# A state-space scan kernel on one Trainium2 core: a fourth product buffer, a later addition, fewer products in PSUM, and fp8 weights rounded once

## The chip, the cores and the metric

The kernel runs on one core of a Trainium2 chip. The metric is device time in microseconds (us) of one execution, and the number compared is the median of several runs. The engines are named as in the profile: PE is TensorE (matmuls and transposes; PEld its weight loads), DVE is VectorE, ACT is ScalarE, POOL is GpSimd, SP is SyncE, which issues the DMAs here. Each engine takes its instructions in the order in which they were queued for it; they wait for each other through semaphores.

## What is computed

The input is x of shape (4, 64, 64, 96) in float32. Four layers follow each other.

- Layer 0 adds to x a two-dimensional selective scan (SS2D) of the group-normalized x: a projection to 192 channels and a gate, a 3x3 depthwise convolution with SiLU, then a state-space scan along four directions (rows, columns, and both reversed), and at the end LayerNorm, the gate and a projection back.
- Layer 1 does the same on the real and imaginary parts of the two-dimensional Fourier transform of x (64 x 33 frequencies, 384 inner channels), image by image, transforms back and adds x.
- Layers 2 and 3 treat the pixels as tokens: attention without a softmax (6 heads), and a feed-forward network whose inputs, weights and biases are rounded to an 8-bit float (5 exponent bits, 2 mantissa bits).

The scan is what matters here. For each direction, channel and one of 16 states n it is

```
dA = jnp.exp(dl[..., None] * A)
hst = hst * dA + (dl * ul)[..., None] * bl[:, :, None, :]
y = jnp.einsum('bkdn,bkn->bkd', hst, cl)
```

so a recurrence along the sequence, for every state, and then a sum over the 16 states of h times C.

## The kernel before

**Pieces.** The scan work is cut into phases: two groups of two images each for layer 0 (g0, g1), and four single images for layer 1 (b0 to b3). A phase holds four directions, each cut into segments along the sequence (eight of 512 elements in layer 0; 512, 512, 384, 384 and 320 in layer 1). There are 144 segments, 64 and 80. In a segment, the 16 states are taken four at a time (q from 0 to 3), and within each q come three chunks of 128 channels (c from 0 to 2). So a segment has twelve steps, and the kernel 1728. `scans` (L524) writes them out in a fixed order for PE, DVE, ACT and POOL; nothing reorders them afterwards.

**One step.** A step `st` computes four states' recurrences (scans 0 to 3, each one DVE instruction, L710), multiplies each by C, and adds the four products up in PSUM, together with those of the other q.

- The factors exp(delta*A) come from ACT: for scans 0 and 1 into SBUF, one step ahead (`front_x`), for scans 2 and 3 into PSUM (`front_y`; both through L682).
- The inputs delta*u*B of scans 0 and 1 are scaled by ACT in transposed form (`make_bx`, L646) and turned by PE into PSUM (`transposed`, L678). Those of scans 2 and 3 are made by POOL (`front_b`, L700), one step ahead, in rows 1 and 2 of a tile h of 3 x 512 elements. A ring of three PSUM banks (`room`, L671) serves these tiles.
- The scan writes either over its input in PSUM, and is then called kept, or into a row of h. `Step.kept` (L519) says which: scan 0 always, and scan 3 too in every other step. Kept results are multiplied by C on DVE (`multiply_kept`, L728) into a tile hk, and ACT copies their last column as the state for the next segment (`keep_state`, L735). All others are multiplied on POOL in one instruction of two or three rows (`multiply`, L747, after the state copy of L744), one step later.
- PE adds products up with transposes that accumulate in PSUM (`accumulate`, L757): `add_kept` for hk, and `add_rest` for the rows of h that POOL multiplied. `add_rest` of a step comes two steps later, at the head of that step (L871). `close_chunk` (L783) copies the sum out once the last q is in.

h has three buffers (L698). `front_b` for the next step is queued on POOL in the middle of a step, behind `multiply` of the step before.

The order of a step (L871 to L910), with each call's engine: add_rest of two steps ago (PE); add_kept 3 of the last step (PE); scan 0 (DVE); front_y 2 and front_x of the next step (ACT); multiply_kept 0 (DVE); add_kept 0 (PE); front_y 3 (ACT); multiply of the last step and front_b of the next (POOL); scan 1 (DVE); a slot; transposed 0 of the next step (PE); scan 2 (DVE); a slot; transposed 1 of the next step (PE); scan 3 (DVE), and its multiply_kept if it is kept; a slot.

**Side work.** Everything else is cut into small pieces that the three slots of a step take (L820) at a rate fixed for each phase (`RATES`, L27: 2.85 pieces a step in layer 1). That is the projections and convolutions of later phases (`Block`), the Fourier transforms (L1033, L1089), the outputs of earlier phases, and `tokens` (L1156), which does layers 2 and 3 of an image while the next image is scanned. The last image's tokens run after the scans, in a wider form. `tokens` loads its weights for every image: float32 tiles by DMA (L1183), of which w1, w2, b1 and b2 of each layer are then rounded to fp8 on DVE (L1189); b1 and b2 are turned back to float32 (L1191). Its `norm_all` (L1205) has two buffers for the squares (L1240). The projection loads hold both halves of a weight chunk (`wi`).

**Broadcasts.** B and C are spread over the partitions by DMAs on SP (`fetch_b`, `fetch_c`, L624), once for each q.

Of the kernel before, what the change touches and what calls it, by code (L numbers as in the profile page):

```python
# [7 lines left out]
F32 = mybir.dt.float32  # L8
F16 = mybir.dt.float16
F8 = mybir.dt.float8e5  # L10
AF = mybir.ActivationFunctionType
# [7 lines left out]
NB, HH, WW, CH = 4, 64, 64, 96  # L19
# [3 lines left out]
C, P = 3, 128  # L23
SM = 512
LATE, BURST = "late", "burst"

RATES = [1.6, 2.35, 2.85, 2.85, 2.85, 2.85]  # L27
EXP_LN = "natural_log_exp_and_others"


# [95 lines left out]
class Inputs:  # L126


    def __init__(self, blk, sp, xf, chunks, half, nm, w):
        self.blk, self.sp, self.xf, self.half, self.nm, self.w = blk, sp, xf, half, nm, w  # L130
        self.todo = [
            (c, r, n) for c in chunks for p0, p1 in blk.cfg.parts for r, n in blk.rows_of(p0, p1, half == 0)
        ]
        self.ahead, self.wi = [], {}
        for _ in range(2):
            self.load()

    def load(self):
        if not self.todo:
            return  # L140
        sp, cfg, nc = self.sp, self.blk.cfg, self.blk.nc
        c, r, n = self.todo.pop(0)
        if c not in self.wi:
            t = sp.tile([CH, cfg.KI, 2, cfg.PI], F32, name=f"{cfg.pre}_wi_{self.nm}_{c}", tag=f"wi{self.w}", bufs=2)
            nc.sync.dma_start(out=t, in_=self.blk.w["inw"][:, :, :, c, :])
            self.wi[c] = t
        x = sp.tile(
            [CH, 2, 512], F32, name=f"xi{self.half}_{self.nm}_{c}_{len(self.todo)}", tag=f"xin{self.w}", bufs=3
        )
        nc.sync.dma_start(out=x[:, :, : n * 64], in_=self.xf[:, :, r * 64 : (r + n) * 64])  # L150
        self.ahead.append((self.wi[c], x))
# [6 lines left out]
class Block:  # L158
# [44 lines left out]
    def in_proj(self, out, wi, half, xin, n):  # L203

        cfg = self.cfg
        for i in range(cfg.NI):
            for ki in range(cfg.KI):
                if i or ki:
                    yield
                self.nc.tensor.matmul(  # L210
                    out[i * cfg.PI : (i + 1) * cfg.PI, :n],
                    wi[:, ki, half, :],
                    xin[:, max(i, ki), :n],
                    start=(ki == 0),
                    stop=(ki == cfg.KI - 1),
                )
# [171 lines left out]
    def gated(self, E, g, io, out_proj):  # L388
# [7 lines left out]
        with E.pool(f"{cfg.pre}nm{g}") as sp:  # L396
# [15 lines left out]
            def worker(w):  # L412
# [6 lines left out]
                for b, (r, nr) in blocks:  # L419
# [93 lines left out]
class Step:  # L513


    def __init__(self, z, q, c):
        self.z, self.q, self.c = z, q, c
        self.nm = f"{z.nm}_{q}_{c}"
        self.kept = (0, 3) if (C * q + c) % 2 else (0,)  # L519
        self.hk = {}  # L520
        self.px, self.ay = {}, {}


def scans(tc, ctx, phases, ident):  # L524
# [8 lines left out]
    nc = tc.nc  # L533
# [161 lines left out]
    def front_b(st):  # L695

        S = st.z.S
        st.h = sp.tile([P, 3, SM], F32, name=f"h_{st.nm}", tag="h", bufs=3)  # L698
        for j in range(2):
            nc.gpsimd.tensor_tensor(  # L700
                st.h[:, 1 + j, :S], st.z.du[:, st.c, :S], st.z.b[st.q][:, j, :S], ALU.mult
            )
# [96 lines left out]
    with tc.manual_schedule(engines=IN_ORDER):  # L799
# [43 lines left out]
        for i, st in enumerate(steps):  # L843
# [309 lines left out]
NT = LTOK // P  # L1153


def tokens(E, ins, consts, ident, x1, b, out):  # L1156

# [5 lines left out]
    with E.pool(f"tk{b}") as sp:  # L1163
# [10 lines left out]
        def weights(ly):  # L1174

            nm, w, bufs = f"{b}_{ly}", {}, min(W, 2)
            for name, shape in (
                ("wqkv", [A, 3 * CH]), ("wqt", [CH, A]), ("wff", [CH, CH]), ("bff", [A, CH]),
                ("w1", [CH, 4 * CH]), ("w2", [P, 3, CH]), ("b1", [P, 3]), ("b2", [P, CH]),
            ):  # L1180
                t = w[name] = sp.tile(shape, F32, name=f"{name}_{nm}", tag=name, bufs=bufs)
                src = ins[f"l{ly}_{name}"]
                nc.sync.dma_start(out=t, in_=src.to_broadcast([P, CH]) if name == "b2" else src)  # L1183
# [11 lines left out]
        loads = [weights(ly) for ly in (2, 3)]  # L1195
        ws = [next(loads[0])] + ([next(loads[1])] if W > 1 else [])
# [3 lines left out]
        yield  # L1200
        yield
        for load in loads[: len(ws)]:
            yield from load

        def norm_all(nm):  # L1205

# [8 lines left out]
            for i in range(n + 2):  # L1215
# [146 lines left out]
        for ly in (2, 3):  # L1362
            nm = f"{b}_{ly}"
            if len(ws) < ly - 1:
                ws.append(next(loads[1]))
                yield from loads[1]
            q = ws[ly - 2]
            wq = q["wqkv"]
            if W == 1:
# [34 lines left out]
def build(tc, ins, consts, out):  # L1404
    nc = tc.nc
    with ExitStack() as ctx:
# [31 lines left out]
        x1 = [dram.tile([LTOK, CH], F32, name=f"x1_{b}", tag=f"x1_{b}") for b in range(NB)]  # L1438
        single = [dict() for _ in range(NB)]

        def flip0(E, g):
            yield from blk[0].flip(E, g, pairs[g])

# [17 lines left out]
        def end1(E, b):  # L1461
            io = single[b]
            att = dram.tile([HH, WF, 2 * CH], F32, name=f"att_{b}", tag="att", bufs=NB)
            put = out1(att, b)
            yield from blk[1].gated(
                E, b, io, lambda E, *a: put(E, blk[1], *a)
            )
            yield
            rest = tokens(E, ins, consts, ident, x1[b], b, out)
# [136 lines left out]
```

## Time and profile before

| | us |
|---|---|
| median of the 3 runs shown | 11332.17 (11327.04 to 11333.0) |
| the profiled execution's own time | 11308.41 |
| its span in the profile | 11306.6 |
| ahead of the first scan | 217.2 |
| layer 0 scans, g0 and g1 | 2451.0 and 2444.0 |
| layer 1 scans, b0 to b3 | 1469.6, 1425.7, 1469.0, 1435.2 |
| after the last scan (the tail) | 395.0 |

The profile holds one execution; its mean granted TensorE clock is 0.90 of full speed. In that profile the busy time of an engine is the sum of its instructions, and its share is taken of the span. A group puts together the instructions of one line, engine and tile; behind its busy time and mean duration stands the idle time that the engine had just before them, and what released it. The waits are the same idle times sorted by waiting group and releaser, with total, count and longest. A segment's or phase's length is counted from its first scan to the next one's first scan.

### The profile page before, as it was taken

Reading aid. Unit: us, or ns where it says so; the run is one execution under the profiler, and the core shown is the slowest. Engines: PE = TensorE matmul, PEld = TensorE weight load, DVE = VectorE, ACT = ScalarE, POOL = GpSimd, SP = SyncE. Lnnn points to the kernel's source line nnn. Section 1 sums busy time; section 2 is a strip of 40 time slices with the busy share of each in tenths; the row PEclk is TensorE's granted clock in tenths of the full one; section 3 lists DMA queues with packets and bytes.
Section 4 is the critical chain, followed back from the end, with each engine's and each line's share of the span. In section 5 each row is a group of like instructions: output and inputs, shape, how many; then the busy total and the mean of one; then the engine's idle time right before and its main releaser. Section 6 shows DMA issues by size and latency. Waiting matters only on the chain. (4 is left out here: it accounts for less than half of the span.)

```text
span 11306.6 us, 163986 instructions
## 1 busy us (share of the span) xinstructions
PE 9021.5 (80%) x54944; PEld 6600.5 (58%) x54944; DVE 9899.2 (88%) x10695; ACT 9384.7 (83%) x19648; POOL 9405.2 (83%) x7464
## 2 busy tenths in 40 slices
PE   5678788777888888888899888887788777887775
PEld 2555555556666656656676665665566555665554
DVE  6889999889999998999888798989989889889864
ACT  3779999999888998998778788878888788878853
POOL 2999999989988998998788798878888779888750
PEclk9889999889999999999889899998899888998887
DMA  5655555556666556555543545442244223542242
GB/s 146 144 130 130 133 129 123 155 156 153 156 161 140 129 144 140 134 142 169 156 134 119 136 136 157 150 113 94 92 145 138 93 90 107 158 120 94 82 130 38
DMA packets 1208406, 1468.97 MB, mean 130 GB/s; under 512 B 482759, under 2 KB 1020559, under 8 KB 1149063
## 3 DMA queue, kind: packets, MB, share of 16 engines
q1 hardware_dynamic: 1207559, 1458.48, 47.8%
q8 instruction: 434, 7.11, 0.3%
q14 instruction: 413, 3.38, 0.1%
HBM read 1221.74 MB, written 236.50 MB: 129 GB/s over the span
## 5 line engine op out<-in xcount | busy, mean ns | idle before, releaser
L747 POOL TENSOR_TENSOR h_l<-h_l,bc_l 128x1536 f32<-128x1536 f32 (+2 forms) x1728 | 4567.8, 2643 | 184.0 <-DVE h_l L710 68.1
L700 POOL TENSOR_TENSOR h_l<-du_l,bc_l 128x512 f32<-128x512 f32 (+2 forms) x3456 | 3966.7, 1170 | 770.1 <-PE acc_l L757 718.1
L646 ACT ACTIVATE bx_l<-dut_l,bt_l 128x192 f32<-128x192 f32 (+2 forms) x6272 | 2756.4, 499 | 0.3
L757 PEld LDWEIGHTS acc_l<-ident,h_l 128*128 128x128 f32 (+1 forms) x15840 | 2047.7, 155 | 689.2 <-issue 325.9
L757 PE MATMUL acc_l<-ident,h_l 128*128 128x128 f32 (+1 forms) x15840 | 2326.3, 299 | 135.9 <-POOL h_l L747 135.6
L682 ACT ACTIVATE ax_l<-delta_l,l_alog 128x512 f32<-128x512 f32 (+2 forms) x3456 | 2140.4, 667 | 0.0
L710 DVE TENSOR_TENSOR_SCAN h_l<-b_l,state_l,h_l 128x512 f32<-128x512 f32 (+2 forms) x1263 | 1389.1, 1121 | 114.2 <-ACT b_l L682 106.6
L678 PE MATMUL b_l<-ident,bx_l 128*128 128x128 f32 (+1 forms) x6817 | 1200.5, 295 | 227.1 <-DVE h_l L710 220.2
L678 PEld LDWEIGHTS b_l<-ident,bx_l 128*128 128x128 f32 (+1 forms) x6817 | 842.9, 149 | 829.5 <-DVE h_l L710 476.8
L682 ACT ACTIVATE b_l<-delta_l,l_alog 128x512 f32<-128x512 f32 (+2 forms) x1948 | 1221.0, 627 | 107.7 <-DVE k_l L728 32.0
L710 DVE TENSOR_TENSOR_SCAN b_l<-ax_l,state_l,b_l 128x512 f32<-128x512 f32 (+2 forms) x842 | 956.5, 1136 | 194.1 <-PE b_l L678 191.3
L757 PE MATMUL acc_l<-ident,k_l 128*128 128x128 f32 (+1 forms) x5117 | 836.9, 294 | 334.3 <-DVE k_l L728 320.1
L678 PE MATMUL ab_l<-ident,bx_l 128*128 128x128 f32 x5312 | 900.9, 298 | 246.5 <-DVE h_l L710 237.7
L682 ACT ACTIVATE ab_l<-delta_l,l_alog 128x512 f32<-128x512 f32 x1326 | 913.8, 689 | 149.0 <-DVE h_l L710 70.0
L678 PEld LDWEIGHTS ab_l<-ident,bx_l 128*128 128x128 f32 x5312 | 648.5, 151 | 622.2 <-DVE h_l L710 452.4
L710 DVE TENSOR_TENSOR_SCAN h_l<-ax_l,state_l,b_l 128x512 f32<-128x512 f32 (+2 forms) x841 | 951.2, 1131 | 42.1 <-PE b_l L678 40.4
L710 DVE TENSOR_TENSOR_SCAN h_l<-ab_l,state_l,h_l 128x512 f32<-128x512 f32 x743 | 920.2, 1261 | 73.2 <-ACT ab_l L682 46.7
L728 DVE TENSOR_TENSOR k_l<-b_l,bc_l 128x512 f32<-128x512 f32 (+2 forms) x1460 | 895.4, 613 | 50.2
L757 PE MATMUL acc_l<-ident,hk_l 128*128 128x128 f32 x3976 | 641.3, 296 | 328.3 <-DVE hk_l L728 315.5
L757 PEld LDWEIGHTS acc_l<-ident,k_l 128*128 128x128 f32 (+1 forms) x5117 | 627.3, 150 | 437.2 <-DVE k_l L728 368.7
L297 PE MATMUL pc_l<-pad_l,l_dg 128*128 128x512 f32 (+2 forms) x1656 | 783.9, 561 | 57.2 <-ACT uh_l L275 42.9
L757 PEld LDWEIGHTS acc_l<-ident,hk_l 128*128 128x128 f32 x3976 | 494.1, 152 | 409.7 <-DVE hk_l L728 337.3
(252 smaller groups left out, 15015.4 us busy)
## 6 DMA issues: line engine op xcount, KB each, us to landing
bc_l<-l_xd_l SPq DMA_DIRECT2D x640, 512.0 KB
bc_l<-l_xd_l SPq DMA_DIRECT2D x512, 256.0 KB
bc_l<-l_xd_l SPq DMA_DIRECT2D x128, 1024.0 KB
bc_l<-l_xd_l SPq DMA_DIRECT2D x128, 768.0 KB
us_l<-l_u SPq DMA_DIRECT2D x96, 768.0 KB
l_y<-y_l SPq DMA_DIRECT2D x288, 256.0 KB
yt_l<-l_y SPq DMA_DIRECT2D x264, 192.0 KB
yt_l<-l_y SPq DMA_DIRECT2D x128, 384.0 KB
```

The costliest lines, as they stand in the source:

```text
L297: nc.tensor.matmul(pc[:, : n * 64].rearrange("p (r w) -> p r w", w=64), diag[:, t, :], pad[:, r - p0 + dy : r - p0 + dy + n, dx : dx + 64] ...
L646: nc.scalar.activation(t[:n, b, :, ch], z.dut[:n, b, :, ch], AF.Copy, scale=z.bt[:n, b, m : m + 1])
L678: nc.tensor.transpose(pb[:, t : t + n], st.z.bx[st.q, j][:n, b, st.c], ident[:n, :n])
L682: nc.scalar.activation(out, z.delta[:, st.c, : z.S], AF.Exp, scale=z.blk.A[:, st.c, z.k, n : n + 1])
L700: nc.gpsimd.tensor_tensor(st.h[:, 1 + j, :S], st.z.du[:, st.c, :S], st.z.b[st.q][:, j, :S], ALU.mult)
L710: nc.vector.tensor_tensor_scan(h[:, ::step], a[:, ::step], b[:, ::step], 0.0 if z.first else z.state[st.c][:, n : n + 1], ALU.mult, ALU.add,)
L728: nc.vector.tensor_tensor(hk[:, : z.S], kept_at(st, j), z.c[st.q][:, j, : z.S], ALU.mult)
L747: nc.gpsimd.tensor_tensor(h, h, z.c[st.q][:, 1 : 1 + m, : z.S], ALU.mult)
L757: nc.tensor.matmul(z.acc[st.c][:m, b, :], hc[:, t : t + m], ident, start=(first and b == 0), stop=(last and b == 0), is_transpose=True,)
```

## The change

1. h gets a fourth buffer.
2. `add_rest` of the step two back moves from the head of a step to behind the slot after scan 2, ahead of `transposed` 1. Steps that work on the last q (q = 3) of their segment keep theirs at the head (`older.q == NQ - 1`).
3. `Step.kept` takes scan 3 too when `(3q + c) % (2 * KI) == 1`. KI is 1 in layer 0, which leaves every other step there, and 2 in layer 1, where 3 steps of 12 remain of 6. In the others POOL multiplies the third row.
4. The fp8 weights and biases of layers 2 and 3 are loaded and rounded once, by a new side task `quantized`, the last of the first phase, into tiles that stay. `tokens` takes them from there.
5. Smaller tiles and edits that go with it: `wi` holds one half of a weight chunk; the input tiles `xin` are as long as their longest use; `Ln` of the normalization writes in place in PSUM, not to a tile of its own; `lnq` has one buffer; the weights of layer 3 are loaded without a generator; two waits of a slot in `tokens` become six; the rate in layer 1 is 2.82, not 2.85.

The lines of the scans move up by one (L710 becomes L709, for instance).

```diff
-RATES = [1.6, 2.35, 2.85, 2.85, 2.85, 2.85]
+RATES = [1.6, 2.35, 2.82, 2.82, 2.82, 2.82]
...
-        self.ahead, self.wi = [], {}
+        self.ahead, self.wi, self.most = [], {}, 64 * max(n for _, _, n in self.todo)
...
-            t = sp.tile([CH, cfg.KI, 2, cfg.PI], F32, name=f"{cfg.pre}_wi_{self.nm}_{c}", tag=f"wi{self.w}", bufs=2)
-            nc.sync.dma_start(out=t, in_=self.blk.w["inw"][:, :, :, c, :])
+            t = sp.tile([CH, cfg.KI, cfg.PI], F32, name=f"{cfg.pre}_wi_{self.nm}_{c}", tag=f"wi{self.w}", bufs=2)
+            nc.sync.dma_start(out=t, in_=self.blk.w["inw"][:, :, self.half, c, :])
...
-                    ln = sp.tile([P, 512], F32, name=f"ln_{nm}", tag=f"ln{w}")
-                    nc.scalar.activation(ln[:, :n], pv[:, :n], AF.Ln, bias=self.eps)
-                    nc.scalar.activation(pv[:, :n], ln[:, :n], AF.Exp, scale=-0.5)
+                    nc.scalar.activation(pv[:, :n], pv[:, :n], AF.Ln, bias=self.eps)
+                    nc.scalar.activation(pv[:, :n], pv[:, :n], AF.Exp, scale=-0.5)
...
-        self.kept = (0, 3) if (C * q + c) % 2 else (0,)
+        self.kept = (0, 3) if (C * q + c) % (2 * z.cfg.KI) == 1 else (0,)
...
-        st.h = sp.tile([P, 3, SM], F32, name=f"h_{st.nm}", tag="h", bufs=3)
+        st.h = sp.tile([P, 3, SM], F32, name=f"h_{st.nm}", tag="h", bufs=4)
...
-            if older:
+            if older and older.q == NQ - 1:
                 add_rest(older)
...
             slot(None, hold=long)
+            if older and older.q < NQ - 1:
+                add_rest(older)
             if nxt:
                 transposed(nxt, 1)
...
+def quantized(E, cp, ins, quant):
...
+    shapes = (("w1", [CH, 4 * CH]), ("w2", [P, 3, CH]), ("b1", [P, 3]), ("b2", [P, CH]))
+    with E.pool("qw") as sp:
+        loaded = []
+        for ly in (2, 3):
+            for name, shape in shapes:
+                t = sp.tile(shape, F32, name=f"{name}_{ly}", tag=f"{name}{ly}")
+                src = ins[f"l{ly}_{name}"]
+                nc.sync.dma_start(out=t, in_=src.to_broadcast([P, CH]) if name == "b2" else src)
+                loaded.append((ly, name, shape, t))
+        for _ in range(6):
+            yield
+        for ly, name, shape, t in loaded:
+            keep = cp if name in ("w1", "w2") else sp
+            r = keep.tile(shape, F8, name=f"q{name}_{ly}", tag=f"q{name}{ly}")
+            yield LATE
+            nc.vector.tensor_copy(r, t, saturate=False)
+            if keep is sp:
+                r, q = cp.tile(shape, F32, name=f"k{name}_{ly}", tag=f"k{name}{ly}"), r
+                nc.vector.tensor_copy(r, q)
+            quant[ly][name] = r
+    yield
...
-                ("w1", [CH, 4 * CH]), ("w2", [P, 3, CH]), ("b1", [P, 3]), ("b2", [P, CH]),
...
-            yield w
-            for name in ("w1", "w2", "b1", "b2"):
-                t = w[name]
-                r = sp.tile(list(t.shape), F8, name=f"q{name}_{nm}", tag=f"q{name}", bufs=bufs)
-                yield LATE
-                nc.vector.tensor_copy(r, t, saturate=False)
-                if name in ("b1", "b2"):
-                    nc.vector.tensor_copy(t, r)
-                else:
-                    w[name] = r
...
+            w.update(quant[ly])
+            return w
...
-                    sq = sp.tile([P, Q, CH], F32, name=f"lnq_{nm}_{t0}", tag="lnq0", bufs=2)
+                    sq = sp.tile([P, Q, CH], F32, name=f"lnq_{nm}_{t0}", tag="lnq0")
...
-            [(flip0, 0), (begin0, 1), (gate0, 0), (gate0, 1)],
+            [(flip0, 0), (begin0, 1), (gate0, 0), (gate0, 1), (quant0, 0)],
```

More of the change, by code (lines that the diff above doesn't have):

```diff
@@ L143, in load @@
         if c not in self.wi:
-            t = sp.tile([CH, cfg.KI, 2, cfg.PI], F32, name=f"{cfg.pre}_wi_{self.nm}_{c}", tag=f"wi{self.w}", bufs=2)
-            nc.sync.dma_start(out=t, in_=self.blk.w["inw"][:, :, :, c, :])
+            t = sp.tile([CH, cfg.KI, cfg.PI], F32, name=f"{cfg.pre}_wi_{self.nm}_{c}", tag=f"wi{self.w}", bufs=2)
+            nc.sync.dma_start(out=t, in_=self.blk.w["inw"][:, :, self.half, c, :])
             self.wi[c] = t
         x = sp.tile(
-            [CH, 2, 512], F32, name=f"xi{self.half}_{self.nm}_{c}_{len(self.todo)}", tag=f"xin{self.w}", bufs=3
+            [CH, 2, self.most], F32, name=f"xi{self.half}_{self.nm}_{c}_{len(self.todo)}", tag=f"xin{self.w}", bufs=3
         )
@@ L211, in in_proj @@
                     out[i * cfg.PI : (i + 1) * cfg.PI, :n],
-                    wi[:, ki, half, :],
+                    wi[:, ki, :],
                     xin[:, max(i, ki), :n],
@@ L1153, with tokens @@
 NT = LTOK // P
-def tokens(E, ins, consts, ident, x1, b, out):
+def quantized(E, cp, ins, quant):
+    nc = E.nc
+    shapes = (("w1", [CH, 4 * CH]), ("w2", [P, 3, CH]), ("b1", [P, 3]), ("b2", [P, CH]))
[19 more added lines that the diff above has]
+    yield
+def tokens(E, ins, consts, ident, x1, b, out, quant):
     nc = E.nc
@@ L1178, in weights @@
                 ("wqkv", [A, 3 * CH]), ("wqt", [CH, A]), ("wff", [CH, CH]), ("bff", [A, CH]),
-                ("w1", [CH, 4 * CH]), ("w2", [P, 3, CH]), ("b1", [P, 3]), ("b2", [P, CH]),
             ):
                 t = w[name] = sp.tile(shape, F32, name=f"{name}_{nm}", tag=name, bufs=bufs)
-                src = ins[f"l{ly}_{name}"]
-                nc.sync.dma_start(out=t, in_=src.to_broadcast([P, CH]) if name == "b2" else src)
-            yield w
-            for name in ("w1", "w2", "b1", "b2"):
-                t = w[name]
-                r = sp.tile(list(t.shape), F8, name=f"q{name}_{nm}", tag=f"q{name}", bufs=bufs)
-                yield LATE
-                nc.vector.tensor_copy(r, t, saturate=False)
-                if name in ("b1", "b2"):
-                    nc.vector.tensor_copy(t, r)
-                else:
-                    w[name] = r
-        loads = [weights(ly) for ly in (2, 3)]
-        ws = [next(loads[0])] + ([next(loads[1])] if W > 1 else [])
+                nc.sync.dma_start(out=t, in_=ins[f"l{ly}_{name}"])
+            w.update(quant[ly])
+            return w
+        ws = [weights(ly) for ly in ((2, 3) if W > 1 else (2,))]
         yield
@@ L1199, in tokens @@
         nc.sync.dma_start(out=x, in_=x1.rearrange("(p t) c -> p t c", t=NT))
[L1200 to L1203, printed above, removed]
+        for _ in range(6 if W == 1 else 2):
+            yield
         def norm_all(nm):
@@ L1364, in tokens @@
             if len(ws) < ly - 1:
-                ws.append(next(loads[1]))
-                yield from loads[1]
+                ws.append(weights(3))
             q = ws[ly - 2]
@@ L1439, in build, with quant0 @@
         single = [dict() for _ in range(NB)]
+        quant = {2: {}, 3: {}}
+        def quant0(E, g):
+            yield from quantized(E, cp, ins, quant)
         def flip0(E, g):
@@ L1468, in end1 @@
             yield
-            rest = tokens(E, ins, consts, ident, x1[b], b, out)
+            rest = tokens(E, ins, consts, ident, x1[b], b, out, quant)
             if E.wide > 1:
```

## The prediction

> **What bounds the kernel now.** I read the engine totals first, then the busy time by stage, then who waits for whom, then the groups of the scan's lines, and last the chain of waits in the tail. The first line gives busy time and share of the span by engine. The windows after it are layer 0 (its two groups), then image 0 and image 2 of layer 1, then the tail; the columns are window, length, and busy time with instruction count of PE, PEld, DVE, ACT and POOL.
>
> ```profile
> PE 9021.5 (80%) x54944; PEld 6600.5 (58%) x54944; DVE 9899.2 (88%) x10695; ACT 9384.7 (83%) x19648; POOL 9405.2 (83%) x7464
> ```
> ```profile
> 217.00:2668.00 2451.00, 1878.85 (x10846) 1330.00 (x10846) 2235.99 (x2136) 2200.67 (x4702) 2310.04 (x1711) 0.91 0.55 137
> 2668.00:5112.00 2444.00, 2021.59 (x12850) 1556.70 (x12849) 2271.59 (x2201) 2220.67 (x4766) 2260.54 (x1657) 0.93 0.60 145
> 5112.00:6582.00 1470.00, 1289.69 (x7829) 952.53 (x7828) 1233.57 (x1410) 1152.68 (x2285) 1189.87 (x1013) 0.89 0.49 141
> ...
> 8007.00:9476.00 1469.00, 1161.77 (x7218) 857.55 (x7219) 1322.87 (x1552) 1233.10 (x2565) 1213.62 (x1016) 0.88 0.37 111
> ...
> 10912.00:11307.00 395.00, 238.87 (x1636) 183.57 (x1636) 139.12 (x261) 129.64 (x325) 3.59 (x5) 0.76 0.37 79
> ```
> No engine is the bound everywhere. In layer 0 POOL is busy 4571 of 4895 us (93%) and DVE 4508. In layer 1 (5112 to 10912, 5800 us) DVE is busy 5143 us (89%) and POOL 4821 (83%): POOL sits still for 979 us there. The reader should see in the waits (total, times, longest) what it waits for:
>
> ```profile
> POOL h_l L700 <- PE acc_l L757: 718.1, 419, 7.9
> ...
> POOL state_l L744 <- DVE h_l L710: 278.2, 195, 10.3
> DVE b_l L710 <- PE b_l L678: 257.4, 200, 8.5
> ...
> PE acc_l L757 <- POOL h_l L747: 135.6, 92, 9.4
> DVE ab_l L710 <- PE ab_l L678: 130.5, 84, 6.9
> ```
> POOL's first product of the next step (L700) waits until PE has added up the step two back, because h has three buffers. DVE's own waits are for PE's transposes, and these groups say which scan they hit (after the bar: busy, mean ns, idle before and its releaser):
>
> ```profile
> L710 DVE TENSOR_TENSOR_SCAN b_l<-ax_l,state_l,b_l 128x512 f32<-128x512 f32 (+2 forms) x842 | 956.5, 1136 | 194.1 <-PE b_l L678 191.3
> ...
> L710 DVE TENSOR_TENSOR_SCAN h_l<-ax_l,state_l,b_l 128x512 f32<-128x512 f32 (+2 forms) x841 | 951.2, 1131 | 42.1 <-PE b_l L678 40.4
> ```
> The first is scan 0 (kept in PSUM), the second scan 1. Over all tile names, scan 0 waits 400 us for PE (295 times) and scan 1 waits 78 us (121 times); ACT's exponentials hold scans 2 and 3 for 246 us; POOL holds DVE for 43 us only, 34 of them in layer 0. So POOL's 718 us of waiting is large, but it is not what DVE waits for.
>
> **What the Trainium skill says.** SBUF — State Buffer, "Who interferes with whom": GpSimd and VectorE share one port pair as an exclusive lock; a DVE op with two SBUF inputs, or a cast in a two-port mode, blocks or is blocked for a whole instruction. The trace agrees: the scans, with one SBUF input each, hold 1.26 to 1.28 us at 512 everywhere, while the fp8 casts (L1189, L1191) take up to 1.72 and 2.59 us beside POOL and 0.16 to 0.66 us in the tail, where POOL is idle. GPSIMD Engine Reference, "Elementwise — side-by-side cycle accounting": about 2.6 cycles an element for two inputs against about one on VectorE; the trace has 3453 ns for 1536 elements (2.25 ns each) against 691 ns for 512. Perfetto Trace Analysis, "What 'DMA-bound' means": a queue that is solid with issues is itself a bound; the tail shows that below.
>
> **The change, part by part.** Everything is set against the profiled execution, 11308.4 us (span 11306.6); the median of the runs shown, 11332.2, lies 23.8 us above it, and I carry that offset.
>
> *(a) fp8 weights once.* Twelve casts leave each of images 0, 1 and 2 and the tail, and twelve stand once at the end of layer 0's first group. In layer 1 they cost 15.0 + 12.2 us of DVE (36 instructions) and 11.0 us of waiting for their loads: 38 us, less 9 (a third of 27.2) where they now stand, 29 us. DVE is one of several limits there, so I take two thirds: **-20**; nothing would be the other end. In the tail the loads of w and b are on the chain, in SP's queue ahead of the loads of `at`:
>
> ```profile
> 11066.40 4.33 SPq L1183
> 11070.78 0.43 SPq L1183
> 11071.25 0.43 SPq L1183
> 11071.72 0.43 SPq L1183
> ...
> 11074.90 4.95 SPq L1183
> 11079.89 0.43 SPq L1183
> 11080.32 0.35 issue
> 11080.67 0.34 SPq L1183
> 11081.06 0.42 SPq L1183
> ```
> These pieces sum to 12.1 us, and the pieces after them follow without a gap: **-12**. The eight loads now issue once in layer 0, some 12 us of SP's time ahead of a broadcast (L624) that is asked for three steps, over 18 us, early: nothing.
>
> *(b) One kept product of two goes to POOL, layer 1.* 80 segments of 12 steps; of six steps with two products in PSUM three remain, so 240 steps change (96 at 512, 96 at 384, 48 at 320). DVE loses a multiply (L728) of 691, 557 or 491 ns: 66 + 54 + 24 = 143 us. POOL's multiply grows from two rows to three: 3453-2366, 2634-1818, 2222-1544 ns, 104 + 78 + 33 = 215 us. ACT loses 192 state copies of 146 ns, off the path. What is the multiply worth now? Measured from scan 0 to scan 0, steps with two kept products last 0.41 us longer than the others at 512, 0.25 at 384 and no longer at 320, where PE sets the pace: 96 x 0.41 + 96 x 0.25 = **-63**; the ends are -143 and 0. POOL pays from its 979 idle us, of which 566 were waits for PE that part (d) ends, and after it has 5036 of about 5750. Locally it becomes the bound: a segment of 512 now needs 9 x 6.15 + 3 x 5.07 + 3 x 1.28 = 74.4 us of POOL (6.15 = 3.45 + 0.19 + 2 x 1.255), and seven such segments last less today (67.8, 73.2, 70.7, 72.9, 74.1, 71.4, 69.2 us): **+22**.
>
> *(c) add_rest in the middle of the step.* It issues PE transposes alone, no DMA: 6 to 12, 1.2 us on average, in 9 of 12 steps; the steps that work on the last q keep it at the head. It is moved past the additions of the kept products, side work of two slots and the transpose for the next scan 0, and stands just ahead of the transpose for the next scan 1. I went through the steps one by one. For each I took how much earlier the addition of kept product 0 could start (its start less the end of its DVE multiply, at most the length of add_rest and its wait) and set that against the wait of the next scan 0: 212 of the 400 us go. Then I took what is left of add_rest, less PE's idle time before the second transpose, against the time that transpose now lies ready before scan 1: 249 us come back, as waits of scan 1. The balance is +37; 15 of it falls in 18 segments of layer 0 where POOL is 97 to 100% busy and hides it: **+22**. The ends are -106 (half the gain, no return) and +143 (half the gain, the whole return). The wait that add_rest itself has, for POOL's multiply, is a step old by then; behind it on PE queue that second transpose and a side slot, and scan 1 waits for them.
>
> *(d) The fourth h buffer.* It ends POOL's 718 us of waiting. Direct worth: the 43 us that DVE waits for POOL, and the 136 us that PE's add_rest waits for POOL's multiply. But 125 of those 136 lie in layer 0, where POOL is full and has nothing to give: **-15**; the ends are 0 and -43.
>
> *The rest:* 0. Ln into PSUM is the same two ACT instructions. One buffer for the squares of norm_all costs nothing, since ACT's Square (L1241) already waits for the centring (L1226) that follows the sum of the last squares on DVE. Half-size weight tiles and the rate of 2.82 keep every side task inside its phase.
>
> Sum: -20 - 12 - 63 + 22 + 22 - 15 = **-66**: 11308.4 becomes 11242, and the median 11332 becomes 11266; I say 11265.
>
> **The rivals.** *Scan 1 takes over from scan 0 (slower).* From the end of multiply 0 PE must place kept addition, slot, transpose, slot, add_rest and transpose inside one DVE step: 0.6 + 0.6 + 1.5 + 0.6 us and two slots in 5.46 us at 512 (a step with no side work). It decides once two slots exceed about 2.1 us; a Fourier slot alone is 1.8. At part (c)'s upper end, +143, with the multiply worth 20 instead of 63: -20 - 12 - 20 + 22 + 143 - 15 = +98, 11430. For it: scan 1's slack is under 0.6 us in a quarter of layer 1's steps. Against: the step that loses the transpose for scan 0 was the one that waited. *Relief in full.* DVE's 143 us all count and layer 1's removable waits (148 us) go with no return: -12 - 29 - 143 + 22 - 148 - 15 = -325, 11007. For it: DVE is the busiest; against: PE is over 85% busy in the segments of 320 and 384. *POOL takes the pace.* The multiply is worth nothing, since POOL (5036) now exceeds DVE (5143 - 143 - 38 = 4962) in layer 1: -20 - 12 + 22 + 22 - 15 = -3, 11329.
>
> **How the numbers follow.** Forecast 0.58, scan 1 takes over 0.18, relief in full 0.10, POOL takes the pace 0.14. Range: below, (a) and (b) at their full size with (c) at 0 and (d) at -43, -29 - 12 - 143 + 22 - 43 = -205, 11127, so 11130, which leaves out the relief in full; above, 11390, between the forecast and the slower rival's centre, which leaves out about half of it. A difference of 0.2%, 23 us, is about what can be told from none here. Faster 0.68 (forecast and relief), within 0.2% 0.14, slower 0.18.
>
> **What would show it.** POOL's L700 waits for PE under 60 us in all. Scan 0's waits for PE near 190, scan 1's near 300. The tail near 383 us. Layer 1 near 5740 us with POOL over 87% busy; layer 0 within 20 us of 4895. Wrong if scan 1's waits stay under 150 (then faster), or if DVE begins to wait for POOL's L700 in layer 1 by more than 60 us (then POOL sets the pace).

## The result and the profile after

The changed kernel takes 11374.87 us (median of 6 runs, 11365.44 to 11392.72), the kernel before 11329.6 beside it (6 runs): the ratio is 1.0044, interval 1.0031 to 1.0056. That is 45 us slower, where 66 us faster was forecast. The profiled execution took 11369.2 us, with a span of 11367.4.

The engine totals of the changed kernel:

```profile
PE 9028.8 (79%) x54944; PEld 6657.9 (59%) x54944; DVE 9755.3 (86%) x10419; ACT 9360.9 (82%) x19456; POOL 9616.7 (85%) x7464
```

DVE has lost 144 us of work and POOL gained 211, close to what was worked out; yet the span is longer. The windows of the changed kernel by stage (columns as before: window, length, then PE, PEld, DVE, ACT, POOL) tell where: layer 0 in all, layer 1 in all, the tail.

```profile
215.00:5232.00 5017.00, 3965.16 (x23700) 2953.13 (x23700) 4526.22 (x4348) 4424.61 (x9467) 4573.47 (x3368) 0.90 0.55 137
...
5232.00:10978.00 5746.00, 4702.93 (x29309) 3475.48 (x29308) 4982.56 (x5681) 4756.64 (x9584) 5026.47 (x4063) 0.90 0.41 123
...
10978.00:11367.00 389.00, 237.86 (x1632) 182.52 (x1629) 136.58 (x249) 129.37 (x325) 6.14 (x5) 0.76 0.35 79
```

Layer 0 is 122 us longer than before (5017 against 4895), with the same instructions but for the casts; DVE is busy 19 us more, PE 65, at a clock of 0.90 instead of 0.92. Layer 1 is 53 us shorter (5746 against 5799), the tail 6 us (389 against 395). These are single executions, 61 us apart where the medians are 45 apart. The waits of the changed kernel (total, times, longest):

```profile
PE acc_l L756 <- DVE hk_l L727: 529.3, 416, 8.8
PE acc_l L756 <- DVE k_l L727: 508.7, 471, 5.8
DVE h_l L709 <- PE b_l L677: 322.7, 281, 5.3
...
DVE b_l L709 <- PE b_l L677: 166.3, 173, 4.9
...
POOL h_l L699 <- PE acc_l L756: 142.5, 91, 5.5
```

POOL's 718 us of waiting for the addition have come down to 142.5, and its waits for DVE's scans ahead of the state copy (L743, L744 before) have gone up from 278 to 629 us. DVE waits more too: the line of h_l is scan 1, which now waits longer than scan 0 below it. And PE itself stands idle longer for DVE's kept products, named hk_l and k_l here (it was 315.5 and 320.1 us). The groups of the two scans say the same (after the bar: busy, mean ns, idle before, its releaser); scan 1 stood at 42.1 us before, scan 0 at 194.1:

```profile
L709 DVE TENSOR_TENSOR_SCAN h_l<-ax_l,state_l,b_l 128x512 f32<-128x512 f32 (+2 forms) x853 | 964.6, 1131 | 277.0 <-PE b_l L677 275.0
L709 DVE TENSOR_TENSOR_SCAN b_l<-ax_l,state_l,b_l 128x512 f32<-128x512 f32 (+2 forms) x853 | 966.1, 1133 | 139.6 <-PE b_l L677 138.0
```

Over all tile names, scan 0 waits 264 us for PE (400 before) and scan 1 456 us (78 before). By layer, scan 0 goes from 127 to 77 us in layer 0 and from 273 to 187 in layer 1; scan 1 goes from 29 to 190 and from 48 to 267.

### The profile page after: what moved, and what is told of

It is laid out like the page before. It is cut to its first block, busy times and chain, and to the rows that moved or that the text cites. A ratio compares the mean times of both kernels' runs of the same rounds, so it can differ in the third digit from the quotient of the medians.

```text
span 11367.4 us, 163563 instructions
## 1 busy us (share of the span) xinstructions
PE 9028.8 (79%) x54944; PEld 6657.9 (59%) x54944; DVE 9755.3 (86%) x10419; ACT 9360.9 (82%) x19456; POOL 9616.7 (85%) x7464
## 5 line engine op out<-in xcount | busy, mean ns | idle before, releaser
L746 POOL TENSOR_TENSOR h_l<-h_l,bc_l 128x1536 f32<-128x1536 f32 (+2 forms) x1728 | 4780.9, 2767 | 298.4 <-DVE h_l L709 174.2
L699 POOL TENSOR_TENSOR h_l<-du_l,bc_l 128x512 f32<-128x512 f32 (+2 forms) x3456 | 3963.8, 1169 | 145.9 <-PE acc_l L756 142.5
L756 PE MATMUL acc_l<-ident,h_l 128*128 128x128 f32 (+1 forms) x16656 | 2454.3, 301 | 43.3 <-POOL h_l L746 43.1
L756 PEld LDWEIGHTS acc_l<-ident,h_l 128*128 128x128 f32 (+1 forms) x16656 | 2194.1, 157 | 404.4 <-issue 213.7
L709 DVE TENSOR_TENSOR_SCAN h_l<-b_l,state_l,h_l 128x512 f32<-128x512 f32 (+2 forms) x1389 | 1505.9, 1108 | 113.4 <-ACT b_l L681 102.5
L756 PE MATMUL acc_l<-ident,k_l 128*128 128x128 f32 x4763 | 808.0, 294 | 528.4 <-DVE k_l L727 508.7
L677 PEld LDWEIGHTS b_l<-ident,bx_l 128*128 128x128 f32 (+1 forms) x6886 | 884.0, 152 | 580.3 <-DVE h_l L709 323.8
L709 DVE TENSOR_TENSOR_SCAN h_l<-ax_l,state_l,b_l 128x512 f32<-128x512 f32 (+2 forms) x853 | 964.6, 1131 | 277.0 <-PE b_l L677 275.0
L709 DVE TENSOR_TENSOR_SCAN b_l<-ax_l,state_l,b_l 128x512 f32<-128x512 f32 (+2 forms) x853 | 966.1, 1133 | 139.6 <-PE b_l L677 138.0
L756 PEld LDWEIGHTS acc_l<-ident,k_l 128*128 128x128 f32 x4763 | 559.8, 147 | 864.7 <-DVE k_l L727 615.8
L709 DVE TENSOR_TENSOR_SCAN h_l<-ab_l,state_l,h_l 128x512 f32<-128x512 f32 x804 | 993.3, 1261 | 80.8 <-ACT ab_l L681 50.0
L756 PE MATMUL acc_l<-ident,hk_l 128*128 128x128 f32 x3628 | 608.1, 296 | 549.1 <-DVE hk_l L727 529.3
L756 PEld LDWEIGHTS acc_l<-ident,hk_l 128*128 128x128 f32 x3628 | 427.5, 148 | 801.1 <-DVE hk_l L727 643.1
L727 DVE TENSOR_TENSOR k_l<-b_l,bc_l 128x512 f32<-128x512 f32 (+2 forms) x1345 | 832.7, 619 | 46.2
```

What stands on the lines that cost most here:

```text
L677: nc.tensor.transpose(pb[:, t : t + n], st.z.bx[st.q, j][:n, b, st.c], ident[:n, :n])
L699: nc.gpsimd.tensor_tensor(st.h[:, 1 + j, :S], st.z.du[:, st.c, :S], st.z.b[st.q][:, j, :S], ALU.mult)
L709: nc.vector.tensor_tensor_scan(h[:, ::step], a[:, ::step], b[:, ::step], 0.0 if z.first else z.state[st.c][:, n : n + 1], ALU.mult, ALU.add,)
L727: nc.vector.tensor_tensor(hk[:, : z.S], kept_at(st, j), z.c[st.q][:, j, : z.S], ALU.mult)
L746: nc.gpsimd.tensor_tensor(h, h, z.c[st.q][:, 1 : 1 + m, : z.S], ALU.mult)
L756: nc.tensor.matmul(z.acc[st.c][:m, b, :], hc[:, t : t + m], ident, start=(first and b == 0), stop=(last and b == 0), is_transpose=True,)
```

## The experiments

Theory A: the addition in the middle of the step delays the transpose for scan 1, and this hides a gain of the other parts. Rivals: POOL's third row is what is late (B); the fp8 side task and the smaller tiles (C); the fourth buffer itself (D). All diffs are against the changed kernel, all ratios against the kernel before on the same chip, whose medians there were 11320 to 11330 us. Durations and waits by layer are from single profiles, medians from 4 to 14 runs.

| kernel | place of add_rest | scan 3 kept in layer 1 | h buffers | median us | ratio, interval |
|---|---|---|---|---|---|
| changed | middle | 3 of 12 | 4 | 11374.9 | 1.0044, 1.0031 to 1.0056 |
| e1_head | head | 3 of 12 | 4 | 11264.4 | 0.9948, 0.9935 to 0.9962 |
| e2_kept_old | middle | 6 of 12 | 4 | 11457.3 | 1.0122, 1.0105 to 1.0139 |
| e3_head_kept_old | head | 6 of 12 | 4 | 11309.0 | 0.9992, 0.9983 to 1.0 |
| e4_three | middle | 3 of 12 | 3 | 11754.1 | 1.0388, 1.037 to 1.0407 |
| e5_fp8_only | head | 6 of 12 | 3 | 11305.9 | 0.9988, 0.9979 to 0.9996 |
| e6_head_three | head | 3 of 12 | 3 | 11260.9 | 0.9956, 0.9941 to 0.997 |
| e7_behind_px1 | behind transpose 1 | 3 of 12 | 4 | 11283.5 | 0.997, 0.9958 to 0.9982 |
| e8_two_rows | middle: two rows only | 3 of 12 | 4 | 11349.3 | 1.003, 1.0018 to 1.0041 |
| e9_two_of_twelve | head | 2 of 12 | 4 | 11273.8 | 0.9959, 0.9946 to 0.9971 |
| e10_behind_kept | behind kept product 0 | 3 of 12 | 4 | 11291.8 | 0.997, 0.9961 to 0.9979 |
| e11_mid_layer1 | middle in layer 1 only | 3 of 12 | 4 | 11279.6 | 0.9961, 0.9949 to 0.9974 |
| e12_rate | head, rate 2.85 | 3 of 12 | 4 | 11263.4 | 0.9953, 0.994 to 0.9967 |
| e13_three_rows | middle: three rows only | 3 of 12 | 4 | 11399.5 | 1.0065, 1.0052 to 1.0079 |
| e14_behind_px0 | behind transpose 0 | 3 of 12 | 4 | 11389.2 | 1.0057, 1.0044 to 1.0069 |

### One part undone: e1_head, e2_kept_old, e3_head_kept_old, e4_three

```diff
-            if older and older.q == NQ - 1:
+            if older:
                 add_rest(older)
...
-            if older and older.q < NQ - 1:
-                add_rest(older)
```

> The changed kernel with one part undone: add_rest stands at the head of every step again; the fourth buffer, the fewer kept products and the fp8 weights stay. Theory A (the addition in the middle delays the transpose for scan 1: the profile after has 190 us of scan-1 waits for PE in layer 0 and 267 us in layer 1, against 29 and 48 before): those waits fall back under 120 us in all, scan 0's rise to about 350, layer 0 returns to about 4895 us from 5017, and the time is 11180 to 11260. Rival B (POOL, loaded with the third row and freed of its waits, is what is late): still 11350 or more. Rival C (the new side task and smaller tiles cost the time in layer 0): layer 0 stays near 5017, over 11330.

Measured: 11264.4, just above the range of theory A, and against B and C. Layer 0 returns to 4915 us and not all the way to 4895. Two windows of this kernel, layer 0 and layer 1:

```profile
217.00:5132.00 4915.00, 3943.93 (x23691) 2930.89 (x23692) 4524.18 (x4348) 4420.92 (x9467) 4571.85 (x3367) 0.91 0.56 140
5132.00:10865.00 5733.00, 4722.46 (x29311) 3453.46 (x29309) 4985.51 (x5681) 4751.74 (x9584) 5028.20 (x4064) 0.90 0.41 124
```

and the groups of scans 0 and 1:

```profile
L709 DVE TENSOR_TENSOR_SCAN b_l<-ax_l,state_l,b_l 128x512 f32<-128x512 f32 (+2 forms) x853 | 967.8, 1135 | 249.5 <-PE b_l L677 247.6
...
L709 DVE TENSOR_TENSOR_SCAN h_l<-ax_l,state_l,b_l 128x512 f32<-128x512 f32 (+2 forms) x853 | 963.6, 1130 | 72.9 <-PE b_l L677 71.0
```

The engines have the same work as in the changed kernel within some 20 us; scan 1's waits are 110 us instead of 456, scan 0's 459 instead of 264 (about 350 was expected). The move of add_rest alone costs 110 us: 102 in layer 0, 13 in layer 1 by these profiles. The rest of the change is a gain of 60 us.

```diff
-        self.kept = (0, 3) if (C * q + c) % (2 * z.cfg.KI) == 1 else (0,)
+        self.kept = (0, 3) if (C * q + c) % 2 else (0,)
```

> The changed kernel with the kept products of before in layer 1 (6 steps of 12 with two in PSUM). Theory A (the kept products moved to POOL were a gain, hidden by the cost of the moved addition): slower than the changed kernel by 60 to 140 us, 11435 to 11515, all of it in layer 1. Rival B (POOL's third row is what costs): faster, 11320 or less.

Measured: 11457.3, 82 us slower than the changed kernel, as theory A has it, and by the profiles nearly all of it in layer 1 (5830 against 5746 us); B falls. Both edits together, with the head place of e1_head and the kept products of before:

> The changed kernel with add_rest at the head and the kept products of before: what is left of the change is the fourth buffer and the fp8 weights with the smaller tiles. Theory A: 11270 to 11310 (fp8 weights 20 to 30 us, the buffer 0 to 20). Rival C (side task, tiles) or a cost of the fourth buffer itself: 11340 or more.

Measured: 11309.0, at the upper end of A's range. So the fewer kept products are worth 45 us with add_rest at the head (11309.0 to 11264.4) and 82 with it in the middle; the move costs 148 us with the old kept products.

```diff
-        st.h = sp.tile([P, 3, SM], F32, name=f"h_{st.nm}", tag="h", bufs=4)
+        st.h = sp.tile([P, 3, SM], F32, name=f"h_{st.nm}", tag="h", bufs=3)
```

> The changed kernel with three h buffers, so POOL's next products wait for the addition that now stands late in the step. Theory A (the fourth buffer is what makes the late addition bearable): slower than the changed kernel by 100 us or more, over 11475, with POOL waiting over 1000 us for PE. Rival D (the fourth buffer brings nothing, or costs by letting POOL run beside DVE): within 25 us of 11375, or faster.

Measured: 11754.1, 379 us slower than the changed kernel. The first line of this kernel's waits:

```profile
POOL h_l L699 <- PE acc_l L756: 1247.9, 611, 12.8
```

The later addition holds h longer, and POOL waits it out. The move needs the fourth buffer.

### What is left without the move: e5_fp8_only, e6_head_three, e12_rate, e9_two_of_twelve

e5 takes the head place, the kept products of before and three buffers together; e6 takes the head place and three buffers.

> The changed kernel with add_rest at the head, the kept products of before and three h buffers: of the change only the fp8 weights, the smaller tiles and the rate of 2.82 are left. The kernel with the same and four buffers had a median of 11309 beside 11324 for the kernel before. Theory A (fp8 weights worth about 30 as forecast, the fourth buffer nothing by itself): 11295 to 11315. Theory B (the fp8 weights are worth nothing, since the new side task lengthens the first group as much as it shortens the rest, and the 15 us are the buffer's): 11320 to 11335.

> The changed kernel with add_rest at the head and three h buffers; the fewer kept products and the fp8 weights stay. With four buffers the same had 11264. Theory A (POOL's waits for PE cost DVE nothing while POOL has room): within 15 us of 11264. Theory B (with the third row POOL needs the fourth buffer to stay ahead): 11290 or more, with DVE waiting for POOL over 60 us in layer 1.

Measured: 11305.9 and 11260.9. Both are within 4 us of the same kernels with four buffers (11309.0, 11264.4), so with add_rest at the head the fourth buffer is worth nothing that these runs can tell, and the fp8 weights with the smaller tiles and the rate are worth 14 us (0.9988, interval 0.9979 to 0.9996). In e6 DVE waits 36 us for POOL in layer 1, not over 60. The waits of e6 have the line

```profile
POOL h_l L699 <- PE acc_l L756: 586.8, 339, 6.9
```

and with the fourth buffer, in e1_head, it is down to 1.8 us. So 585 us of POOL's waiting go, and the time stays.

```diff
-RATES = [1.6, 2.35, 2.82, 2.82, 2.82, 2.82]
+RATES = [1.6, 2.35, 2.85, 2.85, 2.85, 2.85]
```

> The kernel with all add_rest at the head (11264) with the rate of before, 2.85 pieces of side work a step in layer 1 instead of 2.82. Theory A (the rate is worth nothing): within 15 us of 11264. Rival (the fp8 weights were worth less in layer 1 than forecast because the lower rate costs): 11245 or less.

Measured: 11263.4 on top of e1's head place; the rate is worth nothing that these runs can tell.

```diff
-        self.kept = (0, 3) if (C * q + c) % (2 * z.cfg.KI) == 1 else (0,)
+        self.kept = (0, 3) if (C * q + c) % (4 * z.cfg.KI - 2) == 1 else (0,)
```

> The kernel with all add_rest at the head (11264) with scan 3 kept in 2 steps of 12 in layer 1, not 3: DVE loses 80 more multiplies (about 48 us), POOL gains 72 us on 5024 of 5733. Theory A (DVE's path still sets the pace, as from 6 to 3, which gave 45 us for 240 multiplies, 0.19 us each): 11240 to 11260. Rival (POOL is now the pace): 11265 to 11310, with DVE's waits for POOL over 60 us in layer 1.

Measured: 11273.8, again on top of e1's head place. A further 80 multiplies off DVE gain nothing; the interval overlaps e1's, so a loss isn't shown either. The time lies in the rival's range, but DVE's waits for POOL in layer 1 go only from 24 to 41 us, under the 60 that the rival named, so neither theory fits. By the profiles DVE's waits there grow on every side: for PE from 507 to 539 us, for ACT from 158 to 173. The exchange is used up at 3 of 12.

### Where the addition may stand: e7_behind_px1, e10_behind_kept, e14_behind_px0, e11_mid_layer1

```diff
-            if older and older.q < NQ - 1:
-                add_rest(older)
             if nxt:
                 transposed(nxt, 1)
+            if older and older.q < NQ - 1:
+                add_rest(older)
```

> The changed kernel with two calls exchanged: add_rest still in the later half of the step, but behind the transpose for scan 1 instead of ahead of it. Theory A (it is the place ahead of that transpose that costs, not that the addition comes later): scan 1's waits for PE fall from 456 us to under 150, scan 0's rise to about 450, and the time is 11245 to 11290. Rival (a later addition costs by itself, PE then having too much between the second transpose and the next addition of a kept product): 11330 or more.

Measured: 11283.5. The groups of scans 0 and 1:

```profile
L709 DVE TENSOR_TENSOR_SCAN b_l<-ax_l,state_l,b_l 128x512 f32<-128x512 f32 (+2 forms) x853 | 967.6, 1134 | 216.4 <-PE b_l L677 214.6
...
L709 DVE TENSOR_TENSOR_SCAN h_l<-ax_l,state_l,b_l 128x512 f32<-128x512 f32 (+2 forms) x853 | 963.6, 1130 | 76.2 <-PE b_l L677 74.0
```

Scan 1's waits are back at 118 us over all names, scan 0's at 392. Two calls exchanged give back 91 of the 110 us: what costs is mainly that add_rest stands ahead of the second transpose, not that it comes late.

```diff
             add_kept(st, 0)
+            if older and older.q < NQ - 1:
+                add_rest(older)
             front_y(st, 3)
...
-            if older and older.q < NQ - 1:
-                add_rest(older)
             if nxt:
                 transposed(nxt, 1)
```

> The changed kernel with add_rest neither at the head nor in the middle but directly behind the addition of kept product 0. Theory A (the head is the right place because PE waits there for DVE's scan 0 and multiply anyway: its idle time ahead of the addition of kept product 0 grew from 610 to 974 us when add_rest left the head; anywhere behind that multiply it lengthens PE's path to the transposes): scan 0's waits for PE rise above the 459 us of the kernel with all at the head, and the time is 11320 to 11450. Rival (only the place between the two transposes costs, since that is what scan 1 waits for): 11250 to 11290.

Measured: 11291.8, a miss for theory A's expectation and next to the rival's range. Two waits of PE in this kernel:

```profile
PE acc_l L756 <- DVE hk_l L727: 672.7, 506, 8.2
PE acc_l L756 <- DVE k_l L727: 658.5, 589, 5.8
```

PE is idle for DVE's products even longer than in the changed kernel (529.3 and 508.7 us), and this kernel is 83 us faster. So PE's idle time ahead of the kept products is not the cost; I had thought that the addition at the head was well placed because it filled that idle time. Scan 0's waits rise to 512 us, as expected, but scan 1's stay at 90.

```diff
                 transposed(nxt, 0)
+            if older and older.q < NQ - 1:
+                add_rest(older)
             more.take(skip=long)
...
-            if older and older.q < NQ - 1:
-                add_rest(older)
             if nxt:
                 transposed(nxt, 1)
```

> The changed kernel with add_rest directly behind the transpose for scan 0, ahead of scan 2's slot and not behind it; the transpose for scan 1 has the same work ahead of it as in the changed kernel. Theory A (what counts is how much PE has to do between the two transposes): within 30 us of 11375, scan 1's waits over 400 us. Theory B (what counts is that the addition falls behind the end of scan 2, from where the second transpose could start; directly behind the first transpose it would run while PE waits for that end): 11280 to 11320, scan 1's waits under 250 us.

Measured: 11389.2, within 14 us of the changed kernel, which speaks for A; scan 1's waits are 333 us, under A's 400 and over B's 250. Other waits are longer: scan 0's are 306 us against 264, and DVE's `L1330`, a cast of the side work, waits 64.8 us for PE against 24.4. What counts is the work between the two transposes, in both of the places tried.

```diff
-            if older and older.q == NQ - 1:
+            if older and (older.q == NQ - 1 or older.z.cfg.KI == 1):
                 add_rest(older)
...
-            if older and older.q < NQ - 1:
+            if older and older.q < NQ - 1 and older.z.cfg.KI == 2:
                 add_rest(older)
```

> The changed kernel with add_rest in the middle in layer 1 alone, and at the head in layer 0. By the profiles of the changed kernel and of the one with all at the head (layer 0 5017 against 4915 us, layer 1 5746 against 5733): Theory A (the cost lies in layer 0, where the longest additions fall in the steps with the least room): 11265 to 11290, layer 0 within 10 us of 4915. Rival (layer 1 pays as well, hidden in one profile by chance): 11300 or more.

Measured: 11279.6, with layer 0 at 4918 us. Layer 1 pays about 15 us for the move (11264.4 to 11279.6, intervals that overlap), layer 0 some 95.

### Which additions cost: e8_two_rows, e13_three_rows

```diff
-            if older and older.q == NQ - 1:
+            if older and (older.q == NQ - 1 or len(older.kept) == 1):
                 add_rest(older)
...
-            if older and older.q < NQ - 1:
+            if older and older.q < NQ - 1 and len(older.kept) == 2:
                 add_rest(older)
```

> The changed kernel with add_rest in the middle only where it has two rows (8 or 6 transposes); with three rows it stands at the head. Theory A (the long additions, which fall in the steps with one kept product, whose time from scan 2 to the next scan 1 is shorter, make the cost): layer 0 returns to within 15 us of the 4915 of the kernel with all at the head, and the time is 11245 to 11290. Rival (any addition there costs in proportion to its length): about two fifths of the 110 us remain, 11300 to 11320.

Measured: 11349.3, outside both expectations: 85 us over e1, of which layer 0 has 26 and layer 1 71 by the profiles. Its complement exchanges the 1 and the 2 in these conditions:

> The changed kernel with add_rest in the middle only where it has three rows; with two rows it stands at the head. All in the middle cost 110 us over all at the head (11375 and 11264), two rows alone in the middle cost 85 (11349). Theory A (the costs add up by length and step): about 25 us over 11264, so 11280 to 11300. Theory B (each mixture brings two additions close together, one in the middle of a step and one at the head of the next, so a mixture costs more than its parts; three rows in the middle are what costs in layer 0): 11340 to 11400, with layer 0 over 4985 us.

Measured: 11399.5, with layer 0 at 5026 us: theory B. The two halves cost 85 and 135 us, the whole 110, so the costs don't add up. In a mixture an addition in the middle of one step is followed at once by one at the head of the next, and the trace of e8 shows a cost of such pairs in layer 1: the two scans 0 whose transpose is made in a step without an addition at its head wait less than in e1 (32 to 21 us and 22 to 15, summed over all segments), the two a step later, behind the pair of additions, wait more (34 to 52 and 47 to 51). The larger part is again at scan 1, in the steps whose second transpose stands behind the addition (3 to 22 us and 6 to 29). That the pairs are the whole of the excess isn't shown: both mixtures also ran at a lower clock, and in layer 1 of e8 PE was busy for 4782 us with the same matmuls, 60 more than in e1, where the time is 71 us longer. In layer 0 the three-row additions carry the cost: e13 has 183 us of scan-1 waits there, the changed kernel 190, e8 57.

## Why the prediction was wrong, step by step

**(a) fp8 weights, forecast -32, measured -14** (e5, with the smaller tiles and the rate). The tail gave 6 us (395 to 389), not 12; in the fifteen profiles that have this edit it lasts 381 to 393. I had counted the pieces of SP's queue that belonged to the eight loads, two of them 4.33 and 4.95 us long. In the changed kernel these loads are gone, but two pieces nearly as long stand in the chain at the loads that stay:

```profile
11131.84 4.52 SPq L1208
...
11139.09 3.71 SPq L1099
```

The second is a load of the inverse transform that took 0.42 us before (L1098). Why some issues take that long, these runs don't show. The new side task also cost more than I set. Its casts in the changed kernel (min, median, max ns; first and last start):

```profile
L1178 DVE CAST kb<-qb x4: 1149/2314/3460, 2672.4 to 2700.4; 128x3 f32<-128x3 fp8e5 x2, 128x96 f32<-128x96 fp8e5 x2
```

The twelve casts take 16.8 us of DVE, against the 9 that I took as a third of layer 1's. The two longest, 3.45 and 3.46 us for 96 and 3 elements a partition, start with a three-row multiply of POOL (3.44 and 3.45 us) and end with it. That agrees with what the Trainium skill says on the shared port (SBUF — State Buffer, "Who interferes with whom"): of a cast in a two-port mode and an instruction of POOL, the one that comes second is blocked for the whole of the other. Layer 0's first group is 16 to 25 us longer than before (2451) in the seven profiles with layer 0's old order, as much as the casts or somewhat more. What layer 1 gained can't be read off: with the kept products of before it lasts 5791 us in e5 and 5806 in e3, against 5799, and the profile of before is itself 24 us faster than its median.

**(b) kept products to POOL, forecast -63 + 22 = -41, measured -45** (e3 to e1). Right in sign and size of the sum; its two terms, the multiply on DVE and the price on POOL, were not measured apart. With the move in place the same edit is worth 82. DVE's waits for PE ahead of scans 0 and 1 do not explain the difference (664 us in e2, 720 in the changed kernel), and its cause stays open.

**(c) add_rest in the middle, forecast +22, measured +110** (e1 to the changed kernel). This is the step that failed, and with it the sign. Its terms, from e1 to the changed kernel: the relief of scan 0 was forecast at 212 of 400 us and is 195 of 459 (54 in layer 0, 141 in layer 1). The return at scan 1 was forecast at 249 and is 347. The same working split by layer gives 91 and 159 us; measured are 163 and 184. So the balance of the waits is not +37 but +152. In layer 0 it is +109, where the time is 102 us longer; in layer 1 it is +43, but DVE's other waits there, for ACT and POOL and in side work, fall by some 29 us, and the time is only 13 us longer.

The term that was mis-sized is the return at scan 1, through "what is left of add_rest": I took the whole advance of kept product 0 off the delay of the second transpose. I lined up the two traces step by step. In layer 0's 320 steps with a three-row addition in the middle, counted from the start of scan 0, kept product 0 is added 0.57 us earlier, but the transpose for the next scan 0 ends only 0.19 us earlier. So the second transpose starts 1.32 us later, counted from the end of scan 2, where my working gives about 0.9, and it has only 1.67 us to spare there on average. Two things hold the first transpose back. It writes into the PSUM bank that scan 1 reads, and in neither trace does it start sooner than 0.05 us after scan 1's end; in 158 of the 320 steps of the changed kernel (114 in e1) it starts within 0.15 us of that end. In the other 162 steps it comes later, behind side work that in part waits for ACT, most of all the transposes of L611; of the advance that is lost before the first transpose starts, these steps hold about two thirds.

The 15 us that I let POOL hide in layer 0 were not hidden either: POOL's idle time there went from 324 us before, and 343 in e1, to 444 after.

**(d) the fourth buffer, forecast -15, measured 0** (e3 against e5, e1 against e6). POOL's wait was indeed not what DVE waited for. I treated it as a part of its own, though; with the move it carries 379 us (e4), so it belongs to (c). The four measured parts sum to -14 - 45 + 110 + 0 = +51, against +45 for the change.

**The signs I named.** POOL's wait under 60: 142.5. Scan 0 near 190 and scan 1 near 300: 264 and 456. The tail near 383: 389. Layer 1 near 5740 with POOL over 87%: 5746 and 87.5%. Layer 0 within 20 us of 4895: 5017, which is where it went wrong. Neither sign that I had called wrong came: scan 1's waits did not stay under 150, and DVE waited 9 us for POOL's L699 in layer 1. I had named no sign for waits of scan 1 above 300. Of the rivals, "scan 1 takes over from scan 0" names the mechanism; at its price of +143 for (c), and 20 for the multiply, it went too far on both. One reading was too narrow: scans that start from a state take 1.26 to 1.28 us at 512, but those of a first segment 1.20 to 1.22.

**The version that beats both.** The head place with the fewer kept products and the fp8 weights takes 11264.4 (e1), or 11260.9 with three buffers (e6); the changed kernel takes 11374.9.

## What to carry to other kernels

On an in-order queue, a piece of work that is moved should be priced at the place where it lands: count what stands behind it until the next deadline, and take off only the time won that reaches that place. Time won ahead of a fixed wait (here a PSUM bank that comes free at a scan's end, or side work that waits for another engine) is lost there in part: 0.57 us became 0.19. A long wait of an engine that is not the bound (718 us of POOL) is no gain to be had, and ending it can cost; an order is better judged by the waits of the engine that sets the pace. Where parts of a change pull in opposite directions, the profile by stage and one run with each part undone show it: a 60 us gain was hidden under a 110 us loss.

## What the runs showed of the hardware

The mean granted TensorE clock differed more from kernel to kernel than between the runs of one, although the matmuls are the same and only their order or the number of buffers differs: 0.902 to 0.907 in the ten runs of e10_behind_kept, 0.895 to 0.898 in e1_head, 0.892 to 0.896 in the changed kernel, 0.885 to 0.890 in e8_two_rows, 0.882 to 0.885 in e13_three_rows and 0.876 to 0.879 in e4_three. It does not follow the time alone: e10_behind_kept is slower than e1_head. In layer 0 PE's busy time for the same matmuls was 3900 us before, 3944 in e1_head and 3965 in the changed kernel; the step from the second to the third, 21 us, is a fifth of the 102 us between them, and no larger than the scatter among kernels with e1's order of layer 0 (3914 us in e5_fp8_only). Whether the clock causes some of these us or goes with the longer waits was not separated.
